# Spreading a logit row over the partitions by two DMAs through DRAM instead of four TensorE transposes

## The chip, the cores and the metric

The kernel runs on one core of one Trainium2 chip. The metric is the device time of one execution in microseconds (us), lower is better. Before the change the median of three runs is 3412.09 us (3411.46 to 3415.26).

## What is computed

The input is a batch of 32 graphs, x of shape (32, 512, 256) in float32, and one adjacency matrix of 512 x 512. Four layers follow each other, and each adds its result to x: `x = x + layer(relu(layernorm(x)))`. A layer is one or two graph attentions:

```python
Wh = h @ W
s_i = Wh @ a1
s_j = Wh @ a2
e = leaky_relu(s_i[:, :, None] + s_j[:, None, :])
e = where(mask, e, -inf)
h_prime = einsum('bij,bjo->bio', softmax(e), Wh)
```

Layers 0 and 1 have one head of 256 features, layer 2 has four heads of 64, and layer 3 is a multilayer perceptron with two attentions in it, the first (512 features) without a mask, the second (256) with one. Per graph that makes eight matrices of attention weights of 512 x 512: one each in layers 0 and 1, four in layer 2, two in layer 3.

## The kernel before

`fast` (L34) does all the work that is timed; `general` is a fallback behind a flag that these inputs do not set. The 512 nodes of a graph lie as 4 tiles of 128 partitions (`NT` = 4).

One attention runs in stages. `norm_t` normalises (DVE, with GpSimd for the power -0.5) and transposes the tile on TensorE into `hT`. `values` (L210; layers 2 and 3 have their own loops at L314 and L353) multiplies by the weights, which carry three extra columns per head, and ScalarE takes the exponential of these columns (L219, L321, L361). So the node tile `v` holds the features, scaled by the first of the exponentials, and beside them two logit terms in exponential form, T and R. With them a weight is a maximum instead of an exponential of a leaky relu: `w[j, i] = max(R[i], T[j]) * mask[j, i]`. T[j] is one number per partition, but R[i] has to run along the free axis and be the same on all partitions. `weights` (L239) makes that row R: four TensorE transposes of a column of `v`, broadcast to 128 x 128 (L243), fill one PSUM bank `r`; then DVE writes the four tiles of `w` from it (L247 with mask, L251 without). `aggregate` (L257, matmuls on L259) multiplies `w` with `v`; a column of ones gives the denominator, whose reciprocal (L263) DVE takes, and ScalarE scales with it while it empties the bank.

In the first attention of layer 3 (L371 to L383) ScalarE writes two forms of each result (`q` and `y`, L379 and L380), `elu2_plus1` (L283) runs DVE (L285), ScalarE (L286) and GpSimd (L287) on them, and `y` is transposed back on TensorE (L387), 16 transposes for the four node tiles, after all four tiles have been averaged. DVE adds the result to `oT` (L390).

The order of the work: each batch element is a Python generator that yields between steps. Four of them (`NS` = 4) are live at a time, started 20 rounds apart (`LEAD`, L45), and stepped in turn (L436), so a round is one step of each stream. The framework turns this order into one instruction list per engine, with some local reordering, and each engine takes its own list in order. In the steady part of the built program the order repeats every four batch elements. PSUM is one pool of 8 banks, used by everything on TensorE. SBUF buffers rotate by tag: `y` has 8, `w` has 5. SP issues every DMA: 32 loads of x (L64), 32 stores (L421), and the weights at the start. The store of a batch element waits on SP for the last GpSimd addition of that element (L412), and the load behind it on SP waits for the store to land, since it fills the same buffer.

Of the kernel before, what the change touches and what calls it, by code (L numbers as in the profile page):

```python
# [33 lines left out]
def fast(ctx, tc, flag, x, adj, w0, a0, w1, a1, w2, a2, mlp1_w, mlp1_b, mlp2_w, mlp2_b,  # L34
# [12 lines left out]
    const = ctx.enter_context(tc.tile_pool(name="const", bufs=1))  # L47
    work = ctx.enter_context(tc.tile_pool(name="work", bufs=2))
    psum = ctx.enter_context(tc.tile_pool(name="psum", bufs=1, space=bass.MemoryType.PSUM))

    def bank():
        return psum.tile([P, N], FP, tag="b", name="b", bufs=8)
# [29 lines left out]
    def project(dst, block, kt, a_cols):  # L82

        ft, n = a_cols.shape[1], a_cols.shape[2]
        for k in range(kt):
            p = bank()
            for f in range(ft):
                nc.tensor.transpose(p[:, f * P:(f + 1) * P], block(k, f), ident)
            wT = work.tile([P, N], FP, tag="y", name="wT", bufs=8)
            nc.scalar.copy(wT[:, :ft * P], p[:, :ft * P])  # L90
            q = bank()
            for f in range(ft):
                nc.tensor.matmul(
                    q[:, :n], wT[:, f * P:(f + 1) * P], a_cols[:, f, :], start=(f == 0), stop=(f == ft - 1)
                )
            d = dst(k)
            nc.vector.tensor_copy(d, q[:, :n] if len(d.shape) == 2 else q[:, :n].rearrange("p (h c) -> p h c", c=3))
# [43 lines left out]
    W1 = load_w(w1, a1, 0.01, "W1")  # L141
    CH = D + 3
    W2 = const.tile([P, KF, NH, CH], FP, name="W2")
    raw2 = work.tile([P, KF, F], FP, tag="y2", name="raw2", bufs=4)
# [60 lines left out]
    def note(e):  # L205

        c = next(noted)
        nc.vector.tensor_reduce(seen[:, c:c + 1], e, AX.XY, OP.max)
# [27 lines left out]
            yield  # L236
        return o

    def weights(r_col, t_col, masked=True):  # L239

        r = bank()
        for t in range(NT):
            nc.tensor.transpose(r[:, t * P:(t + 1) * P], r_col(t).to_broadcast([P, P]), ident)  # L243
        wt = work.tile([P, NT, N], FP, tag="w", name="w", bufs=5)
        for j in range(NT):
            if masked:
                nc.vector.scalar_tensor_tensor(  # L247
                    wt[:, j, :], r, t_col(j), maskT[:, j, :], op0=OP.max, op1=OP.mult
                )
# [39 lines left out]
    def layer0(xt):  # L289
        v, wt = yield from plain((yield from norm_t(xt)), W0)  # L290
        for t0 in range(0, NT, 2):
            r, q = pair(), pair()
# [18 lines left out]
    def layer2(xt):  # L311
        hT = yield from norm_t(xt)
        v = work.tile([P, NT, NH, CH], FP, tag="v2", name="v2", bufs=2)
        for t in range(NT):  # L314
            ps = bank()
            for k in range(KF):
                nc.tensor.matmul(  # L317
                    ps[:, :NH * CH], hT[:, k, t * P:(t + 1) * P], W2[:, k, :, :], start=(k == 0), stop=(k == KF - 1)
                )
            pv = ps[:, :NH * CH].rearrange("p (h c) -> p h c", c=CH)  # L320
            nc.scalar.activation(v[:, t, :, D:], pv[:, :, D:], AF.Exp)  # L321
            nc.vector.tensor_tensor(
                v[:, t, :, :D], pv[:, :, :D], v[:, t, :, D:D + 1].to_broadcast([P, NH, D]), op=OP.mult
            )
            if t % 2:
                yield
        note(v.rearrange("p t h c -> p (t h) c")[:, :, D:])
        ys = [pair(), pair()]
        for h in range(NH):
            wt = weights(lambda t: v[:, t, h, D + 2:D + 3], lambda j: v[:, j, h, D + 1:D + 2])  # L330
            yield
            p = bank()
            for t in range(NT):
                aggregate(p[:, t * (D + 1):(t + 1) * (D + 1)], wt, t, lambda j: v[:, j, h, :D + 1])
            pv = p[:, :NT * (D + 1)].rearrange("p (t c) -> p t c", c=D + 1)
            r = reciprocal(pv[:, :, D:])
            for i in range(2):
                nc.vector.tensor_tensor(
                    ys[i][:, :, h * D:(h + 1) * D], pv[:, 2 * i:2 * i + 2, :D],
                    r[:, 2 * i:2 * i + 2, :].to_broadcast([P, 2, D]), op=OP.mult  # L340
                )
            yield
        for i in range(2):
            y, q = ys[i], pair()
            nc.scalar.activation(q, y, AF.Exp)
            nc.scalar.activation(y, y, AF.Relu)
            add_elu(xt[:, 2 * i:2 * i + 2, :], y, q)
        yield

    def layer3(xt):  # L350
# [15 lines left out]
                )  # L366
            yield
        note(v[:, :, F:F + 3])
        wt = weights(lambda t: v[:, t, F + 2:F + 3], lambda j: v[:, j, F + 1:F + 2], masked=False)
        yield  # L370
        ys = []  # L371
        for t in range(NT):
            y, q = pair(), pair()
            for c, n in ((0, F + 1), (1, F)):
                ps = bank()
                aggregate(ps[:, :n], wt, t, lambda j: v[:, j, c * (F + 3):c * (F + 3) + n])
                if c == 0:
                    rd = reciprocal(ps[:, F:F + 1])
                nc.scalar.activation(q[:, c, :], ps[:, :F], AF.Exp, scale=rd)  # L379
                nc.scalar.activation(y[:, c, :], ps[:, :F], AF.Relu, scale=rd)  # L380
            elu2_plus1(y, q)
            ys.append(y)
            yield  # L383
        for f in range(KH):
            p = bank()
            for t in range(NT):
                nc.tensor.transpose(  # L387
                    p[:, t * P:(t + 1) * P], ys[t].rearrange("p a f -> p (a f)")[:, f * P:(f + 1) * P], ident
                )
            nc.vector.scalar_tensor_tensor(oT[:, f, :], p, -1.0, oT[:, f, :], op0=OP.add, op1=OP.add)  # L390
            if f % 2:
                yield
        rT = yield from linear_t(oT, WM2, b2, "rT")
        v, wt = yield from plain(rT, WHA)
        for t0 in range(0, NT, 2):
            y, q = pair(), pair()
# [489 lines left out]
```

## Time and profile before

One execution was profiled.

| | us |
|---|---|
| median of 3 runs | 3412.09 |
| profiled execution, its own time | 3417.93 |
| its span, first to last instruction | 3416.2 |
| TensorE (PE) busy | 3314.6 |
| VectorE (DVE) busy | 1700.9 |
| ScalarE (ACT) busy | 1380.6 |
| GpSimd (POOL) busy | 571.7 |
| mean granted TensorE clock | 0.977 of full speed |

A row of the grouped view reads: line, engine, operation, tiles written and read, shape and count; then busy time, mean length of one in ns, and the idle time of the engine just ahead of these instructions with what ended it. Matmuls overlap in the pipeline, so the busy time of a group is less than its count times its mean; start to start a transpose takes 145.7 us / 1024 = 0.142 us. A matmul in float32 stands twice in the trace, a transpose once: for example the 65-column aggregations of layer 2 are 32 x 4 x 16 = 2,048 in the program and 4,096 in the trace.

### The profile page before, as it was taken

To read this page: it belongs to the slowest core of one execution; us is meant where nothing else is said; L and a number is where in the kernel's file an instruction comes from. 1 tells how busy PE (TensorE), PEld (TensorE's weight loads), DVE (VectorE), ACT (ScalarE), POOL (GpSimd) and SP (SyncE) were. 2 spreads that over 40 slices of the span, in tenths; PEclk is the share of its full clock that TensorE was granted. 3 is DMA by queue.
4 is the path that set the end of the run, shared out by engine and by line. 5 is a ranking of instruction groups with operands and counts; after the bars stand their busy time and mean duration, and the time that the engine had idled before them with its cause. 6 is when DMAs were issued, how large, how long until landed. Compare 5 with 4: busy or idle time off the path is not lost.

```text
span 3416.2 us, 44221 instructions
## 1 busy us (share of the span) xinstructions
PE 3314.6 (97%) x17265; PEld 2750.0 (80%) x17265; DVE 1700.9 (50%) x4422; ACT 1380.6 (40%) x3281; POOL 571.7 (17%) x583
## 2 busy tenths in 40 slices
PE   6899999999999999999999999999999999999997
PEld 5688888788887887878878888788888788887875
DVE  3554563554644655446544455454653545635542
ACT  2234434444334434344334443444434444344433
POOL 0111111211112111121111121112201111112111
PEclk8899999999999999999999999999999999999999
DMA  2000000000000000000000000000000000000000
GB/s 80 1 1 13 13 1 13 13 13 13 1 13 13 13 13 1 13 19 7 13 13 1 25 7 7 13 1 25 13 1 13 11 16 13 1 13 7 7 7 14
DMA packets 41606, 40.67 MB, mean 12 GB/s; under 512 B 5296, under 2 KB 40624, under 8 KB 41392
## 3 DMA queue, kind: packets, MB, share of 16 engines
q1 hardware_dynamic: 41392, 37.77, 3.6%
q8 instruction: 140, 2.29, 0.3%
q14 instruction: 74, 0.61, 0.1%
HBM read 20.99 MB, written 16.78 MB: 11 GB/s over the span
## 4 chain that ended last, share of the span: by engine, by line
PE 87%; DVE 6%; ACT 3%; POOL 3%; issue 1%; DMA 0%; SPq 0%; POOLq 0%; ACTq 0%; DVEq 0%
PE b L259 43%; PE b L357 13%; PE b L234 11%; PE b L216 8%; PE b L317 3%; PE b L198 3%; PE b L243 3%; PE b L387 1%; DVE xn L190 1%; POOL y L287 1%; DVE st L182 1%; DVE x L281 1%; POOL rs L186 1%; PE b L405 1%; DVE y L280 1%
## 5 line engine op out<-in xcount | busy, mean ns | idle before, releaser
L259 PE MATMUL b<-v,w 128*128 128x257 f32 (+2 forms) x9216 | 1657.9, 337 | 19.2 <-DVE w L247 16.9
L259 PEld LDWEIGHTS b<-v,w 128*128 128x128 f32 x9216 | 1457.2, 194 | 218.5 <-issue 44.0
L247 DVE SCALAR_TENSOR_TENSOR w<-b,v,maskT 128x512 f32<-128x512 f32 x896 | 609.2, 744 | 37.3 <-PE b L243 37.3
L287 POOL TENSOR_TENSOR y<-y 128x512 f32<-128x512 f32 x192 | 243.4, 1268 | 1799.2 <-ACT y L286 1566.7
L263 DVE RECIPROCAL rden<-b 128x1 f32<-128x1 f32 (+1 forms) x640 | 101.9, 166 | 756.2 <-PE b L259 755.4
L357 PE MATMUL b<-WFC,oT 128*128 128x259 f32 (+1 forms) x2048 | 466.4, 380 | 0.0
L357 PEld LDWEIGHTS b<-WFC,oT 128*128 128x128 f32 x2048 | 381.9, 189 | 62.5 <-issue 8.1
L190 DVE TENSOR_SCALAR xn<-x,mv,rs 128x256 f32<-128x256 f32 x512 | 190.8, 432 | 153.1 <-POOL rs L186 153.1
L216 PE MATMUL b<-W,hT 128*128 128x259 f32 x1024 | 263.4, 402 | 2.1 <-ACT hT L199 2.0
L182 DVE BATCH_NORM_STATS2 st<-x 128x6 f32<-128x256 f32 x512 | 194.4, 406 | 98.3 <-POOL x L308 67.1
L234 PE MATMUL b<-hT,WM 128*128 128x512 f32 x512 | 240.8, 593 | 0.0
L234 PE MATMUL b<-oT,WM 128*128 128x512 f32 x512 | 232.2, 596 | 0.5 <-DVE oT L390 0.5
L216 PEld LDWEIGHTS b<-W,hT 128*128 128x128 f32 x1024 | 195.4, 200 | 34.2 <-ACT hT L199 7.3
L295 ACT ACTIVATE y<-b,rden 128x256 f32<-128x256 f32 x128 | 60.8, 475 | 395.6 <-DVE rden L263 395.6
L379 ACT ACTIVATE y<-b,rden 128x256 f32<-128x256 f32 x256 | 123.2, 481 | 222.7 <-DVE rden L263 173.1
L199 ACT ACTIVATE hT<-b 128x512 f32<-128x512 f32 x256 | 142.3, 595 | 143.7 <-PE b L198 142.5
L221 ACT ACTIVATE v<-b,v 128x256 f32<-128x256 f32 x384 | 182.5, 475 | 12.5
L234 PEld LDWEIGHTS b<-oT,WM 128*128 128x128 f32 x512 | 95.8, 191 | 95.4 <-issue 87.5
L285 DVE TENSOR_SCALAR y<-y 128x512 f32<-128x512 f32 x192 | 82.4, 429 | 178.5 <-ACT y L379 142.4
L364 ACT ACTIVATE v<-b,v 128x256 f32<-128x256 f32 x256 | 121.5, 475 | 117.8 <-PE b L357 113.6
L198 PE MATMUL b<-ident,xn 128*128 128x128 f32 x1024 | 145.0, 283 | 19.1 <-DVE xn L190 19.1
L286 ACT ACTIVATE y<-y,minus 128x512 f32<-128x512 f32 x192 | 138.8, 723 | 57.3 <-DVE y L285 41.4
(99 smaller groups left out, 2892.8 us busy)
## 6 DMA issues: line engine op xcount, KB each, us to landing
x<-in_x_dram SPq DMA_DIRECT2D x32, 512.0 KB, 3.8
out_dram<-x SPq DMA_DIRECT2D x32, 512.0 KB, 2.9
adj<-in_adj_dram SPq DMA_DIRECT2D x1, 1024.0 KB, 8.1
WM<-in_L_gnn_mlp_w_dram SPq DMA_DIRECT2D x2, 512.0 KB, 5.4
WFC<-in_L_gnn_W_fc_dram SPq DMA_DIRECT2D x2, 512.0 KB, 5.7
W<-in_L_gnn_W_dram SPq DMA_DIRECT2D x2, 256.0 KB, 7.8
raw<-in_L_gnn_W_dram SPq DMA_DIRECT2D x1, 256.0 KB, 5.6
WHA<-in_L_gnn_W_hand_dram SPq DMA_DIRECT2D x1, 256.0 KB, 6.2
```

The lines of the kernel that those rows point to most:

```text
L182: nc.vector.bn_stats(st[:, t, :], xt[:, t, :])
L190: nc.vector.tensor_scalar(xn[:, t, :], xt[:, t, :], mv[:, t, 0:1], rs[:, t:t + 1], op0=OP.subtract, op1=OP.mult)
L198: nc.tensor.transpose(p[:, t * P:(t + 1) * P], xn[:, t, k * P:(k + 1) * P], ident)
L199: nc.scalar.activation(hT[:, k, :], p, AF.Relu)
L216: nc.tensor.matmul(ps[:, :F + 3], hT[:, k, t * P:(t + 1) * P], w[:, k, :], start=(k == 0), stop=(k == KF - 1))
L221: nc.scalar.activation(v[:, t, :F], ps[:, :F], AF.Copy, scale=pj)
L234: nc.tensor.matmul(p, w[:, k, f * P:(f + 1) * P], inT[:, k, :], start=(k == 0), stop=(k == kt - 1))
L247: nc.vector.scalar_tensor_tensor(wt[:, j, :], r, t_col(j), maskT[:, j, :], op0=OP.max, op1=OP.mult)
L259: nc.tensor.matmul(p, wt[:, j, t * P:(t + 1) * P], rhs(j), start=(j == 0), stop=(j == NT - 1))
L286: nc.scalar.activation(q, q, AF.Exp, bias=minus1)
L287: nc.gpsimd.tensor_tensor(r, r, q, op=OP.add)
L357: nc.tensor.matmul(ps[c][:, :n], oT[:, k, t * P:(t + 1) * P], WFC[:, k, c * (F + 3):c * (F + 3) + n], start=(k == 0), stop=(k == KH - 1),)
```

## The change

Row R is no longer made on TensorE. A new function `spread` writes the column R of `v` to a small DRAM tile, element by element (the SBUF side is one float per partition and tile, the DRAM side has the same element order turned, `"t p -> p t"`); in layer 2 it does so for each of the four heads, with one DMA each. `weights` then loads that row of 512 floats from DRAM into an SBUF tile `r` on all 128 partitions with one DMA. Both go over SP. One `yield` stands between `spread` and `weights`, so every attention (every layer 2 as a whole) has one more step.

With it come other edits. `r` leaves PSUM and takes SBUF (tag `r`, 6 buffers). Tag `y` has 6 buffers, the `q` tiles have a tag of their own with 3, and a start-up tile moves to another tag. And in layer 3 the transposes of `y` move: after each node tile t, one yield later, its four transposes follow and DVE adds that tile's columns to `oT`; before, all sixteen came after the fourth tile, by feature block.

```diff
+    dram = ctx.enter_context(tc.tile_pool(name="dram", bufs=1, space=bass.MemoryType.DRAM))
...
-            wT = work.tile([P, N], FP, tag="y", name="wT", bufs=8)
+            wT = work.tile([P, N], FP, tag="y", name="wT", bufs=6)
...
-    def weights(r_col, t_col, masked=True):
-
-        r = bank()
-        for t in range(NT):
-            nc.tensor.transpose(r[:, t * P:(t + 1) * P], r_col(t).to_broadcast([P, P]), ident)
+    def spread(cols):
+
+        n = cols.shape[1]
+        row = dram.tile([n, NT, P], FP, tag=f"row{n}", name=f"row{n}", bufs=NS)
+        with nc.allow_non_contiguous_dma(reason="a column into a row"):
+            for h in range(n):
+                nc.sync.dma_start(row[h].rearrange("t p -> p t"), cols[:, h, :])
+        return row
+
+    def weights(row, t_col, masked=True):
+
+        r = work.tile([P, N], FP, tag="r", name="r", bufs=6)
+        nc.sync.dma_start(r, row.rearrange("t p -> (t p)").partition_broadcast(P))
         wt = work.tile([P, NT, N], FP, tag="w", name="w", bufs=5)
...
-    def pair():
-        return work.tile([P, 2, F], FP, tag="y", name="y", bufs=8)
+    def pair(tag="y"):
+        return work.tile([P, 2, F], FP, tag=tag, name=tag, bufs=6 if tag == "y" else 3)
...
     def plain(hT, w):
         v = yield from values(hT, w)
-        wt = weights(lambda t: v[:, t, F + 2:F + 3], lambda j: v[:, j, F + 1:F + 2])
+        r = spread(v[:, :, F + 2:F + 3].rearrange("p t o -> p o t"))
+        yield
+        wt = weights(r[0], lambda j: v[:, j, F + 1:F + 2])
         yield
...
+        rows = spread(v[:, :, :, D + 2].rearrange("p t h -> p h t"))
+        yield
         ys = [pair(), pair()]
         for h in range(NH):
-            wt = weights(lambda t: v[:, t, h, D + 2:D + 3], lambda j: v[:, j, h, D + 1:D + 2])
+            wt = weights(rows[h], lambda j: v[:, j, h, D + 1:D + 2])
...
-        wt = weights(lambda t: v[:, t, F + 2:F + 3], lambda j: v[:, j, F + 1:F + 2], masked=False)
-        yield
-        ys = []
-        for t in range(NT):
-            y, q = pair(), pair()
+        r = spread(v[:, :, F + 2:F + 3].rearrange("p t o -> p o t"))
+        yield
+        wt = weights(r[0], lambda j: v[:, j, F + 1:F + 2], masked=False)
+        yield
+        for t in range(NT):
+            y, q = pair(), pair("q")
...
             elu2_plus1(y, q)
-            ys.append(y)
-            yield
-        for f in range(KH):
+            yield
             p = bank()
-            for t in range(NT):
+            for f in range(KH):
                 nc.tensor.transpose(
-                    p[:, t * P:(t + 1) * P], ys[t].rearrange("p a f -> p (a f)")[:, f * P:(f + 1) * P], ident
+                    p[:, f * P:(f + 1) * P], y.rearrange("p a f -> p (a f)")[:, f * P:(f + 1) * P], ident
                 )
-            nc.vector.scalar_tensor_tensor(oT[:, f, :], p, -1.0, oT[:, f, :], op0=OP.add, op1=OP.add)
-            if f % 2:
-                yield
+            o = oT[:, :, t * P:(t + 1) * P]
+            nc.vector.scalar_tensor_tensor(
+                o, p.rearrange("p (f c) -> p f c", c=P), -1.0, o, op0=OP.add, op1=OP.add
+            )
+            yield
```

More of the change, by code (lines that the diff above doesn't have):

```diff
@@ L143, in fast @@
     W2 = const.tile([P, KF, NH, CH], FP, name="W2")
-    raw2 = work.tile([P, KF, F], FP, tag="y2", name="raw2", bufs=4)
+    raw2 = work.tile([P, KF, F], FP, tag="hT", name="raw2", bufs=3)
     nc.sync.dma_start(raw2, w2.rearrange("(k p) f -> p k f", p=P))
@@ L291, in layer0 @@
         for t0 in range(0, NT, 2):
-            r, q = pair(), pair()
+            r, q = pair(), pair("q")
             for i in range(2):
@@ L343, in layer2 @@
         for i in range(2):
-            y, q = ys[i], pair()
+            y, q = ys[i], pair("q")
             nc.scalar.activation(q, y, AF.Exp)
@@ L395, in layer3 @@
         for t0 in range(0, NT, 2):
-            y, q = pair(), pair()
+            y, q = pair(), pair("q")
             for i in range(2):
```

## The prediction

> **What bounds the kernel now.** First the busy shares and the clock, then the TensorE groups, then who kept TensorE waiting, then one such wait in order of time.
>
> ```profile
> PE 3314.6 (97%) x17265; PEld 2750.0 (80%) x17265; DVE 1700.9 (50%) x4422; ACT 1380.6 (40%) x3281; POOL 571.7 (17%) x583
> PEclk8899999999999999999999999999999999999999
> ```
>
> TensorE is the bound: 97% busy, everything else at most half. What leaves it is won; what makes it wait is lost.
>
> ```profile
> L259 PE MATMUL b<-v,w 128*128 128x65 f32 x4096 | 502.3, 281 | 13.1 <-DVE w L247 13.1
> L243 PE MATMUL b<-ident,v 128*128 128x128 f32 x1024 | 145.7, 273 | 0.0
> L387 PE MATMUL b<-ident,y 128*128 128x128 f32 x512 | 72.3, 276 | 23.8 <-POOL y L287 23.8
> ```
>
> L243 is what the change takes out: 1,024 transposes in 145.7 us. L387 hardly costs time itself, but TensorE stood idle 23.8 us ahead of it.
>
> ```profile
> PE b L387 <- POOL y L287: 23.8, 24, 2.5
> PE b L198 <- DVE xn L190: 19.1, 5, 6.1
> PE b L259 <- DVE w L247: 16.9, 34, 1.0
> ```
>
> Total us, times, longest. These waits are small because the order puts other streams' matmuls between producer and consumer. L387 is the place where that cover is thin:
>
> ```profile
> 1874.62 0.47 ACT L379 ACTIVATE y<-b,rden 128x256 f32<-128x256 f32 x1
> 1874.97 0.48 ACT L380 ACTIVATE y<-b,rden 128x256 f32<-128x256 f32 x1
> 1875.12 0.43 DVE L285 TENSOR_SCALAR y<-y 128x512 f32<-128x512 f32 x1 [1.33 <-ACT y L379]
> 1875.58 0.72 ACT L286 ACTIVATE y<-y,minus 128x512 f32<-128x512 f32 x1
> 1876.38 1.26 POOL L287 TENSOR_TENSOR y<-y 128x512 f32<-128x512 f32 x1 [3.79 <-ACT v L219]
> 1877.70 0.77 PE L387 MATMUL b<-ident,y 128*128 128x128 f32 x5 [2.51 <-POOL y L287]
> ```
>
> From ScalarE's first touch of the second half to the end of GpSimd's add, four handovers take 3.0 us (1874.62 to 1877.64); the queues of DVE and ScalarE ahead of it come on top.
>
> **What the Trainium skill says.** "DMA: Bandwidth & Descriptors", Rules for kernel authors: a strided last dimension becomes one descriptor per element, and a DMA that reads what another wrote has to be issued after the first one's completion semaphore. So a spread is 512 pieces of 4 bytes, and SP stands still from spread to broadcast. The nearest row is the bias load, 128x4x1 floats, at 3.4 us:
>
> ```profile
> out_dram<-x SPq DMA_DIRECT2D x32, 512.0 KB, 2.9
> A<-in_L_gnn_a_dram SPq DMA_DIRECT2D x8, 0.2 KB, 2.5
> bias<-in_L_gnn_mlp_b_dram SPq DMA_DIRECT2D x1, 2.0 KB, 3.4
> ```
>
> "VectorE: DVE Perf Modes", Why PSUM operands drop a tier: a one-source float32 operation is doubled from SBUF only. The trace agrees (L251 from PSUM 746 ns, L285 from SBUF 429 ns); the two-source L247 (744 ns) should stay. "TensorE: Matmul & The Clock Gate", What's actually happening: an idle TensorE falls to half clock. The trace shows half clock once per four batch elements in the steady part, after short gaps ahead of 65-column matmuls:
>
> ```profile
> 1713.20:1716.60 3.40, 2.33 (x14) 0.87 0.00 0
> 1716.60:1720.00 3.40, 3.40 (x18) 0.50 0.00 0
> 1874.00:1877.40 3.40, 1.19 (x7) 1.00 0.00 0
> ```
>
> (window, length, TensorE busy, clock, DMA.) The 2.51 us wait of the last line did not trigger it, so the link is loose here.
>
> **The change, part by part.** All against the profiled execution, 3418 us; the median shown is 6 lower.
>
> 1. Transposes out: 1,024 x 0.142 = -146 us, all on the bound engine.
>
> 2. Where the cover goes. I took the built program's order and added the TensorE work that stands between two instructions, at start-to-start times of the trace (0.142 a transpose, 0.22 a 257-column and 0.11 a 65-column row, two rows each). Summed over the program before this gives 3320 us against 3315 busy, so the yardstick holds.
>
>  The moved transposes (now L399). Before, only the fourth tile's transposes of a batch element were near their producer: 3.3, 3.8, 5.1 and 3.9 us of other work, repeating every four elements. A chain of 4.3 us against these gives 22 us of waits in all; 23.8 were measured, so 4.3 us is the chain with its queues. After, every tile waits for its own chain, and the 16 distances per four elements are 3.5 7.0 3.5 4.7 3.5 3.5 7.6 7.0 4.1 3.5 5.2 5.2 0.0 7.0 0.0 2.9. The zeros come where the other streams' steps in that round have no matmul (the new spread step, the weights step). Shortfalls against 4.3: 15 us per four elements in the steady part, 89 in all, and 68 at ramp and tail, where few streams are live: 158, less 24 of before: +134 us.
>
> 3. The new path of a row. ScalarE's exponential 0.35, spread 3.4, broadcast 3.1 (256 KB; the 512 KB store lands after 2.9, the x load after 3.8), first tile of w 0.75, the other three behind it: 7.6 us to the first, 9.2 needed ahead of a 65-column aggregation. Cover from the last matmul of v to the first aggregation: layers 0, 1 and 3's second 14.4 to 18.6 us, layer 2's first head 10.0 to 11.6, layer 3's first 10.0 to 13.4. Following SP through one repeat with these times, its waits included, leaves TensorE 0.7 us or more everywhere: 0 in the steady part. At ramp and tail it is not covered (distances 0 to 8.6): 76 us of shortfall, against about 16 before, where the path was 3.3 us long: +60 us. The 19 us in which TensorE waited for w (16.9 and 2.4 on L251) mostly go, since w is now made earlier: -15.
>
>  The spread itself isn't in the trace: a 4-byte write to DRAM. Below, 2.5 us (the A loads, of 64 pieces) is the floor. Above, if each of an engine's 32 pieces costs a read and a write of 47 ns (the mean packet: 3.6% of 16 x 3416 us over 41,392 packets), 2.5 + 3.0 = 5.5. I take 3.4.
>
> 4. DVE. It reaches the first w some 1.5 us before the row lands, on most of the 20 attentions per four elements that start a new row. Behind it wait reciprocals, layernorm and L285 of other streams, and so ScalarE and the banks. DVE has half its time free: 0 for itself, but it lengthens the chain of part 2; a chain of 4.7 instead of 4.3 would cost 32 more, 3.9 would cost 30 less. The unmasked w gets faster, 128 x 0.32 = 41 us of DVE: 0. Without that cover, DVE's stalls would count directly, 30 us per four elements.
>
> 5. SP: 512 more DMAs of 0.4 to 0.6 us and a hold in each pair. Rows queue behind the store that waits for GpSimd and the load that waits for it (73 us over the run): bounded by 73, taken at 0. The engines move 164,000 more packets; at 47 ns that is 14% of 16 engines: 0.
>
> 6. One bank of 8 is free: 0, since no wait of TensorE on a bank is listed. Fewer y buffers: 0; their last user is long done in the order; up to 20. Shorter cover from hT to its matmuls: up to 19 by the same count, which overstated this wait before; +10.
>
> 7. Clock: 16 gaps of over 4 us in the steady part and a dozen at the ends. A half-clock stretch is three windows of 3.4 us and costs 5. From 0 to 28 of them; I take 8: +40, range 0 to 140.
>
> Sum: 3418 - 146 + 134 + 60 - 15 + 10 + 40 = 3501, less 6: 3495; rounded down, because a wait in one place shortens another: 3490.
>
> **Rivals.**
> A, the forecast: moved transposes and ramp eat the gain, 3430 to 3560. Chance 0.52.
> B, the DMA legs are longer (spread 5.5, or rows held on SP): 2.1 us more overruns the 0.7 to 3 us of slack in layer 2 and in layer 3's first attention, eight places per four elements by about 1.5 us: 12 x 8 = 96, and 20 at the ends: 3605, 3560 to 3750. Against it: the bias row. Chance 0.25.
> C, the other side: the waits on L399 overlap. The bare chain is 3.0 us; with 3.4 the shortfalls are 95 less 24 = 71, and ramp 30, no clock loss: 3418 - 146 + 71 + 30 - 19 - 6 = 3348, 3330 to 3405. It decides where added waits stay under 146 + 19 us, 5.2 per batch element. For it: before, most waits were under 1 us. Against it: the zeros in the order leave nothing to overlap. Chance 0.18.
> Within 0.2%, which is what a measurement here can tell from no change: 0.05.
> The range 3365 to 3650 leaves out half of C and part of B.
>
> **What would show it.** Right: L243 gone and TensorE busy near 3170; TensorE waiting for GpSimd at L399 by 130 to 190 us, the largest wait in its list; spread landing near 3.4; DVE waiting for the DMA by hundreds of us, TensorE for w hardly in the steady part. Wrong: L399's wait under 80 (then C); TensorE waiting for w by 100 or more (then B); more than 20 new half-clock stretches.

## The result, and the profile after

| | before | after |
|---|---|---|
| median, us | 3413.68 (4 runs, 3411.46 to 3417.07) | 4594.86 (4 runs, 4594.31 to 4605.74) |
| ratio | | 1.3467, 95% interval 1.3443 to 1.349 |
| span of the profiled execution | 3416.2 | 4593.4 |
| TensorE busy / idle in it | 3314.6 / 101.6 | 3662.4 / 931.0 |
| mean granted TensorE clock | 0.977 | 0.845 |

The changed kernel is slower by a third; 3490 had been forecast, 3650 at most. The busy shares and the clock of the kernel after:

```profile
PE 3662.4 (80%) x16241; PEld 2969.6 (65%) x16241; DVE 1669.2 (36%) x4422; ACT 1365.1 (30%) x3281; POOL 595.8 (13%) x583
PEclk7778888978989789888899888897888887987877
```

The 1,024 transposes are gone (17,265 records became 16,241), and yet TensorE is busy for longer: the clock digits, nearly all 9 before, are mostly 7 and 8. A kernel with the same 16,241 records and a clock of 0.981 (e4 below) is busy for 3174.6 us, so 488 us of the 3662 are the same work at a lower clock (busy time times clock is nearly the same in both, 3114 and 3095 us). The rest of the loss is standing still, 931 us against 102. The chain that ended last, and the waits (total us, times, longest):

```profile
PE b L268 26%; DMA row<-v 25%; DMA r<-row 9%; PE b L370 6%; PE b L235 5%; DVE w L256 3%; PE b L217 3%; POOL y L298 2%; PE b L399 2%; PE b L199 1%; DVE st L183 1%; PE b L328 1%; DVE xn L191 1%; ACT q L297 1%; POOL x L319 1%
```

```profile
DVE w L256 <- DMA r<-row: 1207.6, 127, 22.0
...
PE b L268 <- DVE w L256: 338.3, 82, 21.6
...
PE b L399 <- POOL y L298: 313.9, 63, 19.5
DVE w L260 <- DMA r<-row: 312.8, 31, 18.9
```

Before, the DMA's share of this chain was 0%; now the two DMAs of a row are 34% of it. VectorE stands for 1,520 us (1207.6 + 312.8) in front of w, and TensorE's two largest waits are for w and for the add ahead of the moved transposes. SyncE stands longest at spreads, for a `v` that ScalarE has not made yet, then at broadcasts, for the row, and at the stores:

```profile
SPq L246 <- ACT v L220: 1774.2, 56, 82.1
SPq L252 <- DMA row<-v: 1488.3, 161, 12.3
SPq L435 <- POOL x L426: 798.7, 31, 35.9
```

The DMAs, with the median time from issue to landing in the last column:

```profile
r<-row SPq DMA_DIRECT2D x256, 256.0 KB, 5.1
...
row<-v SPq DMA_DIRECT2D x256, 2.0 KB, 10.6
```

2 KB take twice as long as 256 KB. (The trace has 139,264 more packets under 512 bytes than before, 544 for each of the 256 spreads, so a spread does go out element by element.) One spread shows where. It is issued at 1579.65 us, and the broadcast that waits for it on SyncE goes out at 1588.25 (start, length, instruction):

```profile
1579.65 0.37 SPq L246 DMA_DIRECT2D row<-v  x1
...
1588.25 0.32 SPq L252 DMA_DIRECT2D r<-row  x1
```

The same stretch by windows (last two columns: share of the DMA engines, GB/s):

```profile
1580.50:1581.00 0.50, 0.50 (x4) 0.42 (x3) 0.47 (x4) 0.47 (x2) 0.00 (x0) 1.00 0.52 4
1581.00:1581.50 0.50, 0.50 (x3) 0.25 (x2) 0.00 (x0) 0.27 (x3) 0.36 (x2) 1.00 0.00 0
1581.50:1588.00 6.50, 6.50 (x21) 3.63 (x20) 1.38 (x4) 2.38 (x6) 0.91 (x1) 1.00 0.00 0
1588.00:1590.50 2.50, 2.50 (x14) 1.49 (x12) 0.00 (x0) 0.68 (x2) 0.00 (x0) 1.00 0.00 0
1590.50:1591.00 0.50, 0.50 (x5) 0.44 (x4) 0.00 (x0) 0.50 (x3) 0.00 (x0) 1.00 0.00 0
1591.00:1592.00 1.00, 1.00 (x6) 0.88 (x5) 0.00 (x0) 0.88 (x3) 0.00 (x0) 1.00 0.28 111
1592.00:1593.00 1.00, 1.00 (x4) 0.57 (x4) 0.00 (x0) 0.77 (x3) 0.00 (x0) 1.00 0.63 161
```

All 512 pieces pass the engines within half a microsecond, then nothing moves for 7 us, and only then the spread has landed. In this spread the length is not transfer time. The Trainium skill, "DMA: Bandwidth & Descriptors", Latency and other measured facts, says that the receipt round trip to the target memory dominates a DMA's fixed cost of about 2 us. The place agrees (the wait lies behind the packets), the size does not: 7 us here. The broadcast, too, moves nothing for nearly 3 us after its issue; there the idle stretch lies ahead of the packets.

### The profile page after: what moved, and what is told of

It is laid out like the page before. It is cut to its first block, busy times and chain, and to the rows that moved or that the text cites. A ratio compares the mean times of both kernels' runs of the same rounds, so it can differ in the third digit from the quotient of the medians.

```text
span 4593.4 us, 43143 instructions
## 1 busy us (share of the span) xinstructions
PE 3662.4 (80%) x16241; PEld 2969.6 (65%) x16241; DVE 1669.2 (36%) x4422; ACT 1365.1 (30%) x3281; POOL 595.8 (13%) x583
## 3 DMA queue, kind: packets, MB, share of 16 engines
q1 hardware_dynamic: 213424, 105.44, 12.9%
## 4 chain that ended last, share of the span: by engine, by line
PE 44%; DMA 36%; DVE 8%; POOL 5%; ACT 4%; issue 2%; SPq 1%; POOLq 0%; ACTq 0%; DVEq 0%
PE b L268 26%; DMA row<-v 25%; DMA r<-row 9%; PE b L370 6%; PE b L235 5%; DVE w L256 3%; PE b L217 3%; POOL y L298 2%; PE b L399 2%; PE b L199 1%; DVE st L183 1%; PE b L328 1%; DVE xn L191 1%; ACT q L297 1%; POOL x L319 1%
## 5 line engine op out<-in xcount | busy, mean ns | idle before, releaser
L268 PE MATMUL b<-v,w 128*128 128x257 f32 (+2 forms) x9216 | 2025.2, 387 | 444.5 <-DVE w L256 338.3
L268 PEld LDWEIGHTS b<-v,w 128*128 128x128 f32 x9216 | 1743.2, 234 | 736.1 <-issue 468.6
L256 DVE SCALAR_TENSOR_TENSOR w<-r,v,maskT 128x512 f32<-128x512 f32 x896 | 632.1, 747 | 1207.7 <-DMA r<-row 1207.6
L298 POOL TENSOR_TENSOR y<-y,q 128x512 f32<-128x512 f32 x192 | 248.2, 1293 | 2357.5 <-ACT q L297 2144.3
L393 ACT ACTIVATE q<-b,rden 128x256 f32<-128x256 f32 x256 | 121.4, 474 | 870.8 <-DVE rden L272 826.9
L399 PE MATMUL b<-ident,y 128*128 128x128 f32 x512 | 99.4, 327 | 313.9 <-POOL y L298 313.9
L399 PEld LDWEIGHTS b<-ident,y 128*128 128x128 f32 x512 | 70.1, 165 | 340.1 <-POOL y L298 332.4
L317 ACT ACTIVATE y<-b,rden 128x256 f32<-128x256 f32 x128 | 58.4, 473 | 597.2 <-DVE rden L272 597.2
L319 POOL TENSOR_TENSOR x<-x,y 128x512 f32<-128x512 f32 x64 | 91.6, 1431 | 950.5 <-ACT y L317 552.5
L222 ACT ACTIVATE v<-b,v 128x256 f32<-128x256 f32 x384 | 180.8, 476 | 11.1
L306 ACT ACTIVATE q<-b,rden 128x256 f32<-128x256 f32 x128 | 60.7, 474 | 390.3 <-DVE rden L272 367.5
## 6 DMA issues: line engine op xcount, KB each, us to landing
row<-v SPq DMA_DIRECT2D x256, 2.0 KB, 10.6
```

Of the source, the lines that this page charges most:

```text
L222: nc.scalar.activation(v[:, t, :F], ps[:, :F], AF.Copy, scale=pj)
L256: nc.vector.scalar_tensor_tensor(wt[:, j, :], r, t_col(j), maskT[:, j, :], op0=OP.max, op1=OP.mult)
L268: nc.tensor.matmul(p, wt[:, j, t * P:(t + 1) * P], rhs(j), start=(j == 0), stop=(j == NT - 1))
L298: nc.gpsimd.tensor_tensor(r, r, q, op=OP.add)
L319: nc.gpsimd.tensor_tensor(xr, xr, r, op=OP.add)
L399: nc.tensor.transpose(p[:, f * P:(f + 1) * P], y.rearrange("p a f -> p (a f)")[:, f * P:(f + 1) * P], ident)
```

## Is it the wait for the row, or the traffic, or the moved transposes?

**f1: everything issued, nothing waited for.** The later transposes (e1, below) and all spreads and broadcasts, but the broadcast reads a constant row.

```diff
-        nc.sync.dma_start(r, row.rearrange("t p -> (t p)").partition_broadcast(P))
+        nc.sync.dma_start(r, mlp1_b.partition_broadcast(P))
```

> The run with the transposes one tile later (4189), but the broadcast loads a fixed row of DRAM (the bias of the first perceptron layer) instead of the spread's row. Spreads and broadcasts are all still issued; left out is that the broadcast waits for the spread and that R is right. Theory W (the wait for the spread's landing is the loss): 3300 to 3450, and the spreads still take about 10 us to land. Theory L (the load that 131,072 small writes put on the DMA engines and the memory is the loss): over 3800.

Measured: 3220.11 us, ratio 0.9418 (0.9404 to 0.9433), clock 0.992.

```profile
PE 3154.9 (98%) x16241; PEld 2610.1 (81%) x16241; DVE 1692.3 (53%) x4422; ACT 1388.4 (43%) x3281; POOL 589.7 (18%) x583
```

With the same 512 DMAs on the same queue TensorE is at 98%. SyncE's issue time, the packets and the buffers are not the loss; the wait for the row's arrival is. f1 takes that wait away in two places at once: VectorE's, 1,486 us in e1 and 1.1 us here, and SyncE's, which no longer holds a broadcast until its spread has landed. The next section tells the two apart as far as the runs do.

**e4: the transposes taken out and nothing put in** (the kernel before, r a constant tile).

```diff
-        r = bank()
-        for t in range(NT):
-            nc.tensor.transpose(r[:, t * P:(t + 1) * P], r_col(t).to_broadcast([P, P]), ident)
+        r = ones
```

> The kernel before without the 1,024 transposes that make the row: row R is a constant of ones in SBUF, so the weights are computed from a wrong row (left out: the row). Nothing takes its place. If the transposes are worth what the sum said, 3414 - 146 - up to 20 = 3248 to 3268; if they hid in other waits of TensorE, above 3330.

Measured: 3276.07 us, ratio 0.9598 (0.9582 to 0.9614): the transposes are worth about 137 us. The time is 8 us above the range expected.

**e2: the moved transposes alone** (the changed kernel with the row made by four transposes again, in the step that uses it, and without the added step).

```diff
-        r = work.tile([P, N], FP, tag="r", name="r", bufs=6)
-        nc.sync.dma_start(r, row.rearrange("t p -> (t p)").partition_broadcast(P))
+        r = bank()
+        for t in range(NT):
+            nc.tensor.transpose(r[:, t * P:(t + 1) * P], r_col(t).to_broadcast([P, P]), ident)
```

> The changed kernel with the row made by four TensorE transposes again and without the extra step: layer 3's moved transposes and the buffer counts are what remains of the change. Theory D: within 1% of the kernel before, 3400 to 3450; the cover of these transposes is 3.5 to 10.5 us in this order, so their waits stay under 40 us. Theory T: still over 3800.

Measured: 3435.46 us, ratio 1.007 (1.0053 to 1.0087).

```profile
PE b L385 <- POOL y L288: 62.3, 44, 3.3
```

On their own they cost 0.7%, with 62 us of waits at their place, where under 40 had been expected. In the changed kernel the same wait is 314 us.

**e1: the moved transposes one tile later**, so that an averaging of the next tile lies between the add and its transposes (`turn` holds the four transposes of a tile and VectorE's add behind them).

```diff
             elu2_plus1(y, q)
             yield
-            p = bank()
-            for f in range(KH):
...
+            if done is not None:
+                turn(*done)
+                yield
+            done = (y, t)
+        yield
+        turn(*done)
+        yield
```

> The changed kernel, with the transposes of layer 3's node tile t put behind the averaging of tile t+1. By the built order their cover grows from 0.0 to 7.6 us to 8.8 us and more in the steady part. Theory D (the two DMAs are slow, and what waits for them stops VectorE and then TensorE): the 314 us at these transposes shrink, but a good part comes back as TensorE waiting for w, since the row is no earlier: 4250 to 4550. Theory T (the moved transposes without cover are the main loss): most of the 1180 us is gone, under 3800.

Measured: 4189.19 us, ratio 1.228 (1.2259 to 1.23).

```profile
PE b L268 <- DVE w L256: 424.7, 53, 23.3
...
PE b L391 <- POOL y L298: 40.3, 8, 7.6
```

The 314 us wait fell to 40 and 406 us went, 61 more than theory D allowed and far less than theory T. But the spread still lands after 10.9 us, and the wait for w rose from 338 to 425.

## Is it SyncE's list, or the place of the steps?

**e8: ScalarE issues the spreads**, so that SyncE no longer stands in front of them.

```diff
-                nc.sync.dma_start(row[h].rearrange("t p -> p t"), cols[:, h, :])
+                nc.scalar.dma_start(row[h].rearrange("t p -> p t"), cols[:, h, :])
```

> The changed kernel with the spreads issued by ScalarE instead of SP, so that SP is held only by broadcasts. If the loss is mainly that pairs queue on SP (one spread must land before the next may even start), the time falls below 4100. If it is mainly the 10.6 us of each spread itself, 4300 to 4600.

Measured: 4512.18 us, ratio 1.3183 (1.3139 to 1.3227); the spread still lands after 10.7 us, and VectorE still waits 1,422 us for the broadcasts (1176.1 and 245.5). Taking the spreads off SyncE's list won 83 us of the 1,181, net of what their issue costs ScalarE; the broadcasts still stand on SyncE, each until its row is there.

**f4: e1 with three steps between spread and broadcast** (two more `yield` behind each spread).

> The run with the transposes one tile later (4189), spread still in 512 pieces of 4 bytes, but three steps instead of one between spread and broadcast. The cover from the last matmul of v to the aggregation grows from 9 to 15 and more to 18 to 22 us. Theory W: the path of 0.4 + 10.6 + 5.1 + 0.8 = 17 us is now mostly covered in the steady part: 3550 to 3800. If broadcasts queue on SP behind spreads of other streams, so that more steps don't help: over 3950.

Measured: 4234.54 us, ratio 1.2382 (1.2363 to 1.2401), no gain on e1.

```profile
DVE w L256 <- DMA r<-row: 1199.3, 135, 15.9
...
PE b L199 <- DVE xn L191: 307.5, 73, 13.0
...
PE b L268 <- DVE w L256: 112.1, 43, 14.9
```

TensorE waits less for w (112 us against 425 in e1) and about as much more for `xn` (308 against 19), the layernorm that stands behind w on VectorE: here the stall of VectorE's list came out at whoever was next in it.

By the yardstick of the prediction (matmul work of the built order between v and the first use of w, medians; it is a count of the order, not a reading of a trace) the cover is 19.7 us in the layers with one masked head, 19.6 in layer 2 and 22.1 in layer 3's first attention, where it was 16.8, 11.0 and 11.1 in the changed kernel. The way of a row takes about 16.4 us in f4 (0.35 + 10.4 + 4.9 + 0.75, medians). By this count most rows should have been in time for TensorE, and yet it is idle for 768 us (4239.3 - 3471.5), and VectorE stands 1,400 us for rows (1199.3 and 201.1). So the count misses something. It has no place for a row that queues on SyncE behind another stream's, nor for what VectorE's own stalls delay.

**g1: f4 with the spreads on ScalarE** (the edits of f4 and e8 together).

> As f4 (layer-3 transposes a tile later, three steps between spread and broadcast, pieces of 4 bytes), with the spreads issued by ScalarE, which makes the columns, so that SyncE holds the broadcasts, loads and stores alone. Theory SyncE's order: in f4 the extra steps brought nothing because each broadcast stood on SyncE behind spreads of other graphs that waited for ScalarE (1,546 us) and then waited for its row itself (1,478 us). With those gone three steps of about 3.5 us cover the 11 us landing: SyncE's wait for rows under 400 us, VectorE's wait for the broadcasts under 400 us, time 3,300 to 3,600 us. Rival, landing too long for any of these orders: the waits stay within a third of f4's (over 900 us on VectorE) and the time above 4,000 us.

Measured: 4047.14 us, ratio 1.1857 (1.1839 to 1.1875); VectorE's two waits for the broadcasts 1105.1 and 132.5 us. The spread lands after 9.9 us in the median and 20.5 at most.

```profile
SPq L252 <- DMA row<-v: 3078.7, 183, 62.6
```

The numbers named for the rival came. Taking the spreads off SyncE's list is worth 187 us of f4. That the length of the way alone keeps the steps from hiding it is not shown: SyncE stands at a broadcast for up to 62.6 us at once, longer than any landing, so rows can still queue there. What decides is an experiment that shortens the landing and leaves the order alone (h1 and h2 below).

## What makes the landing long?

**e3: 16-byte pieces.** VectorE copies the column into four floats side by side per partition; the spread is 128 pieces of 16 bytes, and the row comes out in the order (partition, tile), which VectorE reads with a stride.

```diff
+        flat = small([n, NT], f"flat{n}")
+        nc.vector.tensor_copy(flat, cols)
+        row = dram.tile([n, P, NT], FP, tag=f"row{n}", name=f"row{n}", bufs=NS)
...
+            nc.sync.dma_start(row[h], flat[:, h, :])
...
+        r = r.rearrange("q (p t) -> q t p", t=NT)
```

> The changed kernel with the column first copied by VectorE to a tile of 4 floats per partition, so that the spread is 128 pieces of 16 bytes instead of 512 of 4 bytes; VectorE reads the row in the other element order. Theory D1 (the spread's time is paid per piece written to DRAM): it lands 4 times sooner above a floor of about 2.5 us, near 4.5, and the time falls to 3500 to 3800. Theory D2 (a small write to DRAM that is read back has a fixed price): it still lands near 10 us and the time stays at 4500 to 4700.

Measured: 3892.47 us, ratio 1.1413 (1.1394 to 1.1432).

```profile
row<-flat SPq DMA_DIRECT2D x256, 2.0 KB, 2.3
```

```profile
L258 DVE SCALAR_TENSOR_TENSOR w<-r,v,maskT 128x512 f32<-128x512 f32 x896 | 1019.3, 1181 | 480.4 <-DMA r<-row 480.3
```

The same 2 KB land in 2.3 us, sooner than theory D1 had it, while the time stays 92 us above its range. A price comes elsewhere: read with a stride of 16 bytes, w takes 1181 ns in place of 747. But e3 changes three things at once (number, size, place), so the pieces had to be taken one by one.

**g2: the same 512 pieces to four places.** A first try, f2 (3219.44 us), wrote to the four places with nothing that read them, and its trace has no landing times. So g2: in f1's setting, with a small DMA behind each spread that reads one element and so waits for it: packed (`row`), every 64 bytes (`wide`), every 512 bytes (`apart`), and into the partitions of an SBUF tile (`inner`).

```diff
+                row = dram.tile([NT, P, 16], FP, tag="wide", name="wide", bufs=NS)
+                nc.sync.dma_start(row.rearrange("t p c -> p t c")[:, :, 0], cols[:, 0, :])
...
+        nc.sync.dma_start(got, row)
```

> As f1 (VectorE reads a constant row, so R's value and the wait for it are left out), with the spreads of a single row going in turn to four places: packed in DRAM (row, 4-byte pieces side by side), every 64 bytes in DRAM (wide), every 512 bytes in DRAM (apart), and into each partition of an SBUF tile at every eighth byte (inner, no DRAM). One small DMA behind each reads an element of it, so that the landing shows. Theory S, pieces that share a small stretch of DRAM wait for each other: packed 10 to 11 us, wide 5 or less, apart about 3, inner about 2.5. Theory P, each small write to DRAM is paid wherever it goes: packed, wide and apart all 9 to 12 us, inner about 2.5. Theory N, the number of pieces is paid wherever they go: all four 9 to 12 us.

Measured: 3214.39 us, a single run. SyncE's list at the start (start, length, instruction):

```profile
55.61 0.38 SPq L261 DMA_DIRECT2D row<-v  x1
...
64.30 0.31 SPq L268 DMA_DIRECT2D got<-row  x1
75.46 0.40 SPq L249 DMA_DIRECT2D wide<-v  x1
...
77.37 0.24 SPq L268 DMA_DIRECT2D got<-wide  x1
```

The reader goes out 8.7 us behind the packed spread and 1.9 us behind the wide one. Over all 32 pairs each the shortest distance is 1.85 (wide), 1.78 (apart) and 2.03 us (inner), while none of the 160 packed pairs is under 8.4 us. Longer ones, up to 17 us for the three, can hold time in which SyncE stood elsewhere in its list, so these are only bounds. Neither the number of pieces nor that they are small DRAM writes makes the 10 us: theory S.

**h1: the changed kernel with each element 64 bytes from the next**, pieces, queue, order, waits and SBUF buffers as they were. The broadcast reads the first 2 KB of that place, so it still waits. Two small things differ besides: the places are filled with zeros once at the start, and single rows take 8 places in turn in place of 4 (h3 below comes back to a place only after 12 single rows and still lands late when packed, so the number of places is not the cause).

```diff
-                nc.sync.dma_start(row[h].rearrange("t p -> p t"), cols[:, h, :])
+                nc.sync.dma_start(row[h].rearrange("t p c -> p t c")[:, :, 0], cols[:, h, :])
...
+        return [row[h].rearrange("t p c -> (t p c)")[:N] for h in range(n)]
```

> The changed kernel with one thing other: the spread puts each element of a row 64 bytes from the next in DRAM, not 4. Pieces (512 of 4 bytes), queue, order, waits, buffers and layer-3 transposes are as in the changed kernel. The broadcast reads the first 2 KB of that place, of which every 16th element is the row's and the others are zeros written once at the start, so that it still waits for the landing; R's values are left out. Theory S, pieces that share a small stretch of DRAM wait for each other: spread landing 2 to 3.5 us in place of 10.6, VectorE's wait for the broadcasts under 500 us in place of 1,520, time 3,450 to 3,650 us, about what was forecast for the changed kernel. Rival, the number of pieces: landing above 8 us, time above 4,300 us.

Measured: 3694.87 us, ratio 1.0839 (1.0816 to 1.0861).

```profile
r<-wide SPq DMA_DIRECT2D x256, 256.0 KB, 3.9
...
wide<-v SPq DMA_DIRECT2D x256, 2.0 KB, 2.9
```

```profile
DVE w L266 <- DMA r<-wide: 348.5, 113, 9.7
...
PE b L409 <- POOL y L308: 151.4, 61, 4.9
...
DVE w L270 <- DMA r<-wide: 64.2, 29, 5.7
```

This is the experiment that decides. Placing the same pieces apart takes 900 of the 1,181 us away. VectorE's wait for the broadcasts falls from 1,520 to 413 us (348.5 and 64.2), TensorE's idle time to 273.5 (3686.2 - 3412.7). The time is 45 us above the range expected.

**h2: h1 with the later transposes of e1.**

> As h1, with the layer-3 transposes a tile later (as in e1). R's values are left out as there. If landing length alone made e1 slow, this comes to e6's time or a little less (same order, landing 2.3 us there): 3,330 to 3,450 us, VectorE's wait for the broadcasts under 250 us. If the wait stays over 500 us, something else than the landing holds the rows, and the time is above 3,600 us.

Measured: 3385.77 us, ratio 0.9924 (0.9908 to 0.9941), against 4189 for e1; VectorE's waits 316.1 and 69.3 us, over the 250 expected, TensorE's wait for w 75.2. So the placement is worth 803 us here. It is no kernel to use, since R's values are left out, but it shows what this order takes with a short landing: within 1% of the kernel before. f1, which waits for no spread, lies 166 us below.

**h3: how far apart?** As h1, with the elements of single rows every 4 (`bya`), 8 (`byb`), 16 (`byc`) and 32 bytes (`byd`), and those of layer 2's rows every 64 (`bye`).

> As h1 (R's values are left out), with the single rows going in turn to places with the elements every 8 (byb), 16 (byc), 32 (byd) and 4 bytes (bya), and the rows of layer 2 every 64 bytes (bye). If what counts is how many pieces fall into one stretch of 64 bytes, the landing falls step by step: every 4 bytes 9 to 11 us, 8 bytes 5 to 7, 16 bytes 3.5 to 5, 32 bytes 2.5 to 3.5. If there is one threshold (pieces of one word's write), all three wider ones are alike at 2 to 3 us.

```profile
bye<-v SPq DMA_DIRECT2D x128, 2.0 KB, 3.9
byb<-v SPq DMA_DIRECT2D x32, 2.0 KB, 6.0
byc<-v SPq DMA_DIRECT2D x32, 2.0 KB, 2.8
byd<-v SPq DMA_DIRECT2D x32, 2.0 KB, 2.0
bya<-v SPq DMA_DIRECT2D x32, 2.0 KB, 8.9
```

(3865.80 us, a single run.) For single rows there is no threshold but a slope: 8.9, 6.0, 2.8, 2.0 us for distances of 4, 8, 16 and 32 bytes, the shape expected, most of it a little below the figures expected. Counted in pieces per 64 bytes (16, 8, 4, 2), each one more costs 0.4 to 0.8 us: (8.9 - 6.0) / 8 = 0.36, (6.0 - 2.8) / 4 = 0.8, (2.8 - 2.0) / 2 = 0.4. Writes into one stretch that are taken one after the other would fit, but no run shows it; how long such a stretch is, and which part of the memory does it, these runs do not tell. Nor is distance all: layer 2's rows, the furthest apart, land after 3.9 us. Their four spreads go out together, which the single rows' do not; that this is the reason was not tested. The 16-byte pieces of e3, side by side, land like 4-byte pieces every 16 bytes (2.3 and 2.8 us). That fits the distance of the pieces' starts counting, and not their size, but e3 also has a quarter as many pieces. The Trainium skill, "DMA: Bandwidth & Descriptors", Specifications, gives 512 bytes as the least transfer at full rate, with read-modify-write below. All the pieces here are below, and they land after 2.0 or after 8.9 us, so that limit alone does not tell the two apart.

## Is there a form of the change that is faster than before?

Four more forms of the row, all with the later transposes of e1 and none with packed 4-byte pieces.

**e5: e3 with the later transposes** (the edits of e3 and e1 together).

> Both changes of the earlier runs together: spread in 128 pieces of 16 bytes (it landed after 2.3 us instead of 10.6) and layer 3's transposes one tile later. If the two losses are separate, the 174 us at these transposes go from 3892 and half clock with them: 3600 to 3720. If VectorE, which needs 1181 instead of 744 ns for a tile of w from the turned row and waits 480 us for rows, is behind both, less than half of that: 3780 to 3890.

Measured: 3548.47 us, ratio 1.0398 (1.0377 to 1.0419), landing 2.4 us, TensorE's wait for w 145.5 us. That is below both ranges expected.

**e6: e5 read straight**, so that only the sorting of the row is left out.

```diff
-        r = r.rearrange("q (p t) -> q t p", t=NT)
```

> As e5, but VectorE reads the row as it lies (the element order of R is left wrong: left out is the sorting of the row), so a tile of w takes about 744 ns again. It tells the price of the turned read: if VectorE's longer tiles matter, 100 us and more below e5, near 3400 to 3550; if only the DMA legs matter, within 40 us of e5.

Measured: 3432.49 us, ratio 1.0045 (1.0029 to 1.0061). The strided read costs 116 us; even without it the way of the row eats what the transposes gave.

**f3: the row in order by numbering node p of tile t as 4p + t**, so that TensorE loads every fourth column of w as weights.

```diff
-            nc.tensor.matmul(p, wt[:, j, t * P:(t + 1) * P], rhs(j), start=(j == 0), stop=(j == NT - 1))
+            nc.tensor.matmul(p, wt[:, j, :].rearrange("q (p t) -> q t p", t=NT)[:, t, :], rhs(j), start=(j == 0), stop=(j == NT - 1))
```

> Meant to beat both: spread in pieces of 16 bytes, and node 4p+t on partition p of tile t instead of node 128t+p, so that the row lies in DRAM in the order in which it is used and VectorE reads it straight; TensorE loads every fourth column of w as weights instead. One more step in layer 2, transposes of layer 3 one tile later. Compared with 3432 for the unsorted row: the extra step should take the 79 us of waits in the steady part and some half clock. If the strided weight load costs nothing: 3310 to 3400. If it is slower than the straight one by more than the matmul hides, as VectorE's strided read was, over 3450.

Measured: 4075.62 us, ratio 1.1931 (1.1915 to 1.1947), TensorE 97% busy.

```profile
L269 PEld LDWEIGHTS b<-v,w 128*128 128x128 f32 x9216 | 2234.2, 328 | 120.4 <-issue 49.3
...
PE 3945.3 (97%) x16241; PEld 3469.1 (85%) x16241; DVE 1733.1 (43%) x4582; ACT 1387.0 (34%) x3281; POOL 597.4 (15%) x583
```

The waits are nearly gone (34.7 us for w), the weight load takes 328 ns in place of 198 in e6, and TensorE itself is slower. Its mean granted clock is 0.878, with only 121 us of idle time (4066.0 - 3945.3); why it is so low here was not taken apart.

**e7: one transpose of the whole column**, a ScalarE copy, 512-byte pieces to DRAM, two steps between.

```diff
+        nc.tensor.transpose(p[:m, :P], cols, ident)
+        flat = work.tile([m, P], FP, tag=f"flat{m}", name=f"flat{m}", bufs=2)
+        nc.scalar.copy(flat, p[:m, :P])
+        row = dram.tile([m, P], FP, tag=f"row{m}", name=f"row{m}", bufs=NS)
+        nc.sync.dma_start(row, flat)
```

> The column is turned once on TensorE (one transpose for one attention, one for all four heads of layer 2: 160 instead of 1,024), ScalarE copies the 4 or 16 rows of 128 floats to SBUF, one DMA writes them to DRAM in pieces of 512 bytes, and the broadcast loads them. Two extra steps between instead of one, layer 3's transposes one tile later. If pieces of 512 bytes land as soon as pieces of 16 (about 2.3 us), rows are in time: TensorE 23 us more than without transposes, 3276 + 23 + 20 to 100 for ramp and tail: 3310 to 3400, faster than the kernel before. If two DMAs through DRAM are too slow whatever the pieces, over 3450.

Measured: 3553.63 us, ratio 1.0401 (1.0383 to 1.0418). VectorE waits only 110 us for the broadcasts, and the loss is still there: TensorE is idle for 283 us (3552.2 - 3269.4), 106.1 of them in front of `xn`. So it is a miss, and not for the reason its other branch gave, DMAs that are too slow. What the two emptier steps do to the order was not taken apart further.

**g3: e7 without DRAM**, four broadcasts of 64 KB out of the SBUF tile, one step between.

```diff
-        nc.sync.dma_start(r.rearrange("q (t p) -> q t p", p=P), row.partition_broadcast(P))
+                nc.sync.dma_start(r[:, t * P:(t + 1) * P], flat[k:k + 1, :].rearrange("o (u p) -> o u p", u=1).to_broadcast([1, P, P]))
```

> As e7 (one TensorE transpose turns the column, ScalarE copies it into an SBUF tile, layer-3 transposes a tile later) without the DRAM row: four broadcasts of 64 KB each, one for each tile of 128 nodes, read the SBUF tile itself, one step ahead of w instead of two; a head's broadcast is issued when the head before it is used. Theory: the way is one landing of 4 to 5 us, one step nearly covers it; TensorE busy 3,220 to 3,260 us (256 transposes of a whole column less three quarters of the 1,024), VectorE's wait for the broadcasts under 250 us, time 3,350 us (3,280 to 3,430), below the kernel before. Rival: all pieces of 512 bytes come out of one partition's memory, so that the broadcast takes 8 us or more; VectorE's wait over 500 us and the time above 3,550 us.

Measured: 4079.93 us, ratio 1.1951 (1.1934 to 1.1967), a clear miss: the rival's wait and time came, with a shorter landing than it had. Each broadcast lands after 6.1 us in the median, VectorE waits 1,349 us for them (1049.5 and 299.0), and the DMA engines are busy for 34.4% of the span, against 12.9% in the changed kernel. That all pieces come out of one partition fits; it was not measured by itself.

No kernel here that computes all of the reference is faster than the kernel before.

## Why the prediction was wrong, point by point

1. Transposes out: -146 forecast, about -137 measured (e4). Right.
2. Moved transposes: waits of 158 us forecast. h1, with the order of the changed kernel and a landing near the forecast one (2.9 and 3.4 us), has 151: right for the landing that was assumed. e2 has 62, but in another order, without the added step. With the long landing it is 314, which the forecast did not allow for. The wait does not simply follow VectorE's standing for rows: e8 has 173 us of it with 1,422 us of standing, the changed kernel 314 with 1,520. What else makes it grow stays open. The line of e8:

```profile
PE b L399 <- POOL y L298: 173.0, 62, 11.2
```

3. **The step that failed: "I take 3.4" for the spread, with 5.5 as the upper end. It lands after 10.6 us.** The nearest row was a load into SBUF, where the pieces spread over partitions (g2's `inner`: from 2.0 us); the change writes 512 pieces side by side into 2 KB of DRAM. The upper end priced the pieces by the time they take on the engines, which is half a microsecond in the spread shown; the price lies behind it. The trace before has no such write. It does have another load of 512 single floats into SBUF, `WFCa` at the start, that landed after 6.1 us with other loads in flight, and the forecast passed it over. The broadcast took 5.1 us in place of 3.1.

 With the measured legs the forecast's own count gives 0.35 + 10.6 + 5.1 + 0.75 = 16.8 us against a cover of about 11 in layer 2's first head and layer 3's first attention: 5.8 short, twice per element, 32 elements: 371 us. TensorE's waits for w come to 368 (338.3 and 29.7). That is luck, for they lie elsewhere:

```profile
L268 PE MATMUL b<-v,w 128*128 128x257 f32 x4096 | 1116.3, 429 | 207.5 <-DVE w L256 101.5 <-DVE rden L272 55.5 <-DVE w L260 29.7
L268 PE MATMUL b<-v,w 128*128 128x65 f32 x4096 | 699.3, 345 | 237.0 <-DVE w L256 236.8
```

 Layer 3's first attention (L260) waits 29.7 us where the count gives 186, the masked attentions with one head 101.5 where it gives none, layer 2 with all its heads 236.8 where it gives 186. So the size of this term was wrong, and the count by cover did not hold with the long landing (nor in f4).

 The landing is not the whole of it. With 2.9 us (h1) the kernel takes 3695, still 205 above the forecast. TensorE's idle time there, 273.5 us, is close to what the forecast adds up to (101.6 + 134 + 60 - 15 + 10 = 291), and near it in its two main places (151 at the moved transposes with 158 forecast, 58.5 for w with about 64); its busy time is 3,413 against a forecast of 3,209 (3314.6 - 146 + 40). What is left is term 7, the clock.

4. VectorE's stalls, "0 for itself": wrong for the long landing, since 1,520 us of standing came out as TensorE's waits for w and for `y` at L399, and in f4 for `xn`. With the short landing of h1 VectorE stood for 413 us, and TensorE's idle time was about the forecast's.

5. SyncE, bounded by 73 us of rows behind stores and loads, taken at 0. SyncE stands at the stores for 799 us in the changed kernel, but also for 770 in f1, where TensorE is at 98%, so that is not the loss. What the forecast did not price is broadcasts behind other streams' spreads: 83 us by e8, 187 with more steps (g1). That 83 lies near 73 says nothing. The engines' busy share went from 3.6% to 12.9% (14% more had been forecast), and f1 has no loss with 20.9%: right.

6. Banks and buffers, +10: f1 has these buffers and is 5.8% faster than before; nothing of it shows.
7. Clock, +40 with 140 at most: about 488 in the changed kernel, and 238 in h1 (3412.7 - 3174.6), where the idle time was as forecast. So this is the second term that was mis-sized. In f1, h2, h1 and the changed kernel the clock falls as the idle time grows: 0.992, 0.964, 0.919 and 0.845 with 65, 148, 273 and 931 us. But the sum of the gaps does not set it: g1 has 0.914 with 668 us idle, almost the clock of h1, and f3 has 0.878 with 121. Which gaps, or what else, pull it down stays open.

Rival B had the mechanism, longer DMA legs, and its own sign for it (TensorE waiting 100 us or more for w) came; its 5.5 us was half of what was there. Rival A and rival C both rested on the same short landing.

## What to carry to other kernels

In these runs a DMA that wrote many small pieces side by side into DRAM was priced by how closely the pieces lay, not by bytes, packets or engine time; if the price is not in the trace, leave the range wide open on that side. Look at who stands behind the wait on the same engine: VectorE was busy for 36% of the time and its waits for rows still stopped TensorE, since a late row on VectorE holds up every stream that shares it. Give the clock a term of its own: with the idle time that had been forecast (h1) it took six times the 40 us allowed. And when a count's total fits, see whether its places do.

## What the runs showed of the hardware that was not expected

- 512 writes of 4 bytes, single rows: landing 8.9 us at a distance of 4 bytes, 6.0 at 8, 2.8 at 16, 2.0 at 32 (h3). In the packed spread shown all pieces passed the engines within half a microsecond.
- A broadcast of 2 KB from DRAM to 128 partitions, in the one shown, moves nothing for nearly 3 us after its issue; the medians of its landing run from 3.0 us (h3, behind `byd`) to 6.0 us (e8).
- VectorE's w from a row read with a stride of 16 bytes: 1181 ns in place of 747. A weight load of every fourth column: 328 ns in place of 198.
- A mean granted TensorE clock of 0.878 with TensorE busy for 97% of the span (f3).
